# The scan of sixteen units: in two of them the product with C goes from VectorE to GpSimd

## The chip, the cores and the metric

The kernel runs on one core of a Trainium2 chip, as one program. The metric is the device time of that core in microseconds (us). The engines are named as in the profile: PE is TensorE, DVE is VectorE, ACT is ScalarE, POOL is GpSimd, and SP is the engine that issues the transfers.

## What is computed

The reference is four layers on a tensor of four images, 64 by 64 pixels and 128 channels. Layers 0 and 1 contain a selective scan in four directions over the 4096 pixels of an image; layers 2 and 3 are a graph of neighbours and a neighbourhood attention, and the change doesn't touch them. The scan is

```
def step(h, inp):
    d, u, b, c = inp
    dA = jnp.exp(d[..., None] * A)
    h = dA * h + (d * u)[..., None] * b[:, :, None, :]
    y = jnp.sum(h * c[:, :, None, :], axis=-1)
    return (h, y)
...
_, ys = lax.scan(step, h0, seq)
```

with 16 states `h` for each channel, 128 channels in layer 0 and 256 in layer 1. Everything is in fp32.

## The kernel before

There are twelve scan tasks, one for each image and tile of 128 channels (four in layer 0, eight in layer 1). A task runs over four directions and, in each, over four chunks of 1024 pixels. A chunk holds 128 channels x 16 states, 2048 recurrences, and is cut into sixteen units: a unit is 8 channels x 16 states on the 128 partitions, and 1024 pixels along the free dimension. That makes 256 units a task and 3072 in all. In the loop of `run` a unit `u` takes these steps, each issued some units ahead of the scan:

- `load` (six units ahead, L393): SP issues a transfer of 512 KB that spreads delta times x from DRAM over the states, into `dub` (four buffers).
- `times_b` (three ahead, L398): POOL multiplies `dub` by the repeated B into `dbu` (three buffers). The buffer of `dbu` for unit u+3 is the one that the scan of unit u reads last.
- `decay` (two ahead, L406 and L408): PE spreads delta into `da`, a tile of two banks in PSUM (two buffers), and ACT takes the exponential in place.
- `scan` (L418, L428, L430): DVE runs the recurrence over `da` and `dbu`, in place in `da`. In three of the four chunks of a direction it copies the last column into `state`, from where the next chunk's scan starts. Then it multiplies `da` by the repeated C into `hc` (six buffers, in SBUF). The buffer of `da` comes free with that multiplication.
- `add_up` (L453): for each group of four units PE gathers the four `hc` into the running sum `yps`, one half of the pixels in the slot of the group's last unit and the other half in the next slot.

The order of instructions on each engine is written out by the program as it stands; nothing reorders them later. Between the units, a planner (`Plan` and `Lane`) places two other streams: the preparation of the next chunk (`prepare`: delta, its exact split in three bf16 parts, delta times x; four POOL operations of 1024 columns a chunk) and a side stream of all the convolutions, norms and projections of layers 0 and 1. The planner keeps an estimate of when each of PE, ACT and POOL is free, `at`, charges each unit a fixed amount in `slot` (2.4 us on POOL), and lets a piece of the other streams in where its engine's estimate fits. DVE does almost nothing but the units. A one-off per task, `skip` (L441), is a small tensor-scalar operation on DVE from SBUF to SBUF.

After the last scan the rest of the program (the last image's end of layer 1, then layers 2 and 3) follows.

Of the kernel before, what the change touches and what calls it, by code (L numbers as in the profile page):

```python
# [26 lines left out]
NG = 16  # L27
# [87 lines left out]
class Plan:  # L115
# [37 lines left out]
    def slot(self, u, sums):  # L153
        at = self.at
        self.now = u * UNIT
        self.flush()
        at["PE"] = max(at["PE"], self.now) + 1.1
        at["ACT"] = max(at["ACT"], at["PE"]) + 1.1
        at["POOL"] = max(at["POOL"], self.now - 1.2) + 2.4
        at["PE"] += sums  # L160


# [71 lines left out]


NU = ND * NSTEP * NG
AHEAD = 22


class Scans:  # L240
# [140 lines left out]
    def unit(self, u):  # L381
        n, i = divmod(u, NU)
        step, g = divmod(i, NG)
        jj, j = divmod(g, 4)
        t = self.tasks[n]
        return t, step, jj, j, 4 * j + jj
# [23 lines left out]
    def scan(self, u):  # L410
        nc = self.nc
        t, step, jj, j, g = self.unit(u)
        back = t.steps[step][0] >= 2
        way = slice(None, None, -1) if back else slice(None)
        if g == 0:
            t.states[step] = self.tile("state", 2, shape=(P, NG))
        da, dbu = self.live.pop(("da", u)), self.live.pop(("dbu", u))
        nc.vector.tensor_tensor_scan(  # L418
            da[:, way],
            da[:, way],  # L420
            dbu[:, way],
            0.0 if step % NSTEP == 0 else t.states[step - 1][:, g : g + 1],
            ALU.mult,
            ALU.add,
        )
        if step % NSTEP < NSTEP - 1:
            end = 0 if back else TS - 1
            nc.vector.tensor_copy(t.states[step][:, g : g + 1], da[:, end : end + 1])  # L428
        hc = self.live["hc", u] = self.tile("hc", 6)
        nc.vector.tensor_mul(hc, da, t.prepared[step]["C"])  # L430

    def sum_so_far(self, u, i):

# [43 lines left out]
    def run(self, between):  # L477

        total = NU * len(self.tasks)
        first = self.tasks[0]  # L480
        for _ in self.fetch(first):
            pass
        for _ in self.prepare(first, 0):
            pass
        self.plan.start()
        pieces, fetch = Lane(self.plan, iter(())), iter(())
        for u in range(-6, total):
            if u >= 0:
                self.scan(u)
            if u >= 2:  # L490
                self.keep(u - 2)
            if 0 <= u + 3 < total:
                self.times_b(u + 3)
            if 0 <= u + 2 < total:
                self.decay(u + 2)
            if u >= 0 and u % NG in (2, 3):
                self.sum_so_far(u, u % NG - 2)
            if u >= 0 and u % 4 == 3:
                self.add_up(u, 0)
            if u > 0 and u % 4 == 0:  # L500
                self.add_up(u - 1, 1)
            self.plan.slot(u, (1.6 if u % 4 in (0, 3) else 0.0) + (2.1 if u % NG in (2, 3) else 0.0))
            ahead, rest = divmod(u + AHEAD, NG)
            if rest == 0:
                while pieces.step():
                    pass
                self.plan.flush("prep", "rep")
            if rest == 0 and 0 < ahead < total // NG:
                n, step = divmod(ahead, NU // NG)
                if step == 0:  # L510
                    self.plan.flush("side")
                    fetch = self.fetch(self.tasks[n])
                    for _ in range(self.tasks[n].W.nct):
                        next(fetch, None)
                pieces = Lane(self.plan, self.prepare(self.tasks[n], step))
            next(fetch, None)
            while (pieces.count < rest - 2 or pieces.fits()) and pieces.step():
                pass
            if u >= 0:
                n, i = divmod(u, NU)  # L520
                if self.later:
                    self.later.pop(0)()
                between(n, i)
            if 0 <= u + 6 < total:
                self.load(u + 6)
        self.add_up(total - 1, 1)
        self.keep(total - 1)
        while self.later:
            self.later.pop(0)()
# [508 lines left out]
def scan_layers(tc, C, nb, x_in, d0, s0, d1, s1, out):  # L1038

    nc = tc.nc  # L1040
    with ExitStack() as es:
# [19 lines left out]

        last = {g: group.index(g) * NU - AHEAD - 1 for g in range(1, len(groups))}
        last[len(groups)] = NU * len(tasks) - 16
        lane, current, credit = None, None, 0.0
# [396 lines left out]
def layer2(tc, C, nb, x_in, x_out, d_w, d_rel, d_v):  # L1461
    with ExitStack() as es:
# [11 lines left out]

        with tc.manual_schedule():
            run(each(E.statistics, 0, range(8)))
            E.roots([E.rstd])
            run(each(E.project, 0, range(6)))
            E.edge_row()
            run(each(E.statistics, 1, range(2)))  # L1480
            before = last = None
            for b in range(nb):
# [392 lines left out]
```

## Time and profile before

| | |
|---|---|
| median of 3 runs | 14536.44 us (14521.81 to 14541.9) |
| the profiled execution's own time | 14538.91 us |
| its span, first to last instruction | 14537.1 us |
| the scans, first start to last end | 202 to 11721 us |
| busy in the span: PE, DVE, ACT, POOL | 73%, 85%, 54%, 68% |
| one scan on DVE, with and without a start state | 2350 and 2290 ns |
| one product with C on DVE | 1218 ns |
| one product with B on POOL | 2356 ns |
| one exponential on ACT | 1089 ns |

Busy shares are averages over the whole span; the stage of the scans takes about four fifths of it, and the rest has other limits. In the rows of groups, "idle before" is the time that an engine stood still just ahead of those instructions, with the engine and tile whose completion ended the wait. A wait for several things is put down to the one that came last. In the text, "unit 5" means a unit whose number is 5 modulo 16.

### The profile page before, as it was taken

To read this page: it belongs to the slowest core of one execution; us is meant where nothing else is said; L and a number is where in the kernel's file an instruction comes from. 1 tells how busy PE (TensorE), PEld (TensorE's weight loads), DVE (VectorE), ACT (ScalarE), POOL (GpSimd) and SP (SyncE) were. 2 spreads that over 40 slices of the span, in tenths; PEclk is the share of its full clock that TensorE was granted. 3 is DMA by queue.
4 is the path that set the end of the run, shared out by engine and by line. 5 is a ranking of instruction groups with operands and counts; after the bars stand their busy time and mean duration, and the time that the engine had idled before them with its cause. 6 is when DMAs were issued, how large, how long until landed. Compare 5 with 4: busy or idle time off the path is not lost. (4 is left out here: it accounts for less than half of the span.)

```text
span 14537.1 us, 125468 instructions
## 1 busy us (share of the span) xinstructions
PE 10657.1 (73%) x36776; PEld 2733.4 (19%) x36776; DVE 12418.0 (85%) x10627; ACT 7829.5 (54%) x9243; POOL 9857.4 (68%) x4742
## 2 busy tenths in 40 slices
PE   5777777777767776667766777667777767777999
PEld 1111111111111111111111111111111112223555
DVE  4998899989999999989998999999999925565666
ACT  3665466645655466545655555555555545543555
POOL 4777788878877788778877888888888833341000
PEclk7666676666676766677666776667766678777999
DMA  6888888987889888988888878788787720002000
GB/s 164 215 215 218 202 211 214 222 219 205 210 227 219 208 211 206 228 204 206 211 207 215 204 193 204 194 204 203 195 206 193 194 80 22 25 13 49 13 13 8
DMA packets 854306, 2489.98 MB, mean 171 GB/s; under 512 B 143095, under 2 KB 164863, under 8 KB 845431
## 3 DMA queue, kind: packets, MB, share of 16 engines
q1 hardware_dynamic: 853623, 2481.97, 67.8%
q8 instruction: 295, 4.83, 0.1%
q14 instruction: 388, 3.18, 0.1%
HBM read 2060.21 MB, written 270.27 MB: 160 GB/s over the span
## 5 line engine op out<-in xcount | busy, mean ns | idle before, releaser
L398 POOL TENSOR_TENSOR dbu<-dub,repB 128x1024 f32<-128x1024 f32 x3072 | 7196.1, 2356 | 1649.0 <-DVE da L418 873.9
L418 DVE TENSOR_TENSOR_SCAN da<-da,state,dbu 128x1024 f32<-128x1024 f32 x2304 | 5415.0, 2350 | 376.9 <-ACT da L408 294.3
L408 ACT ACTIVATE da<-da,av 128x1024 f32<-128x1024 f32 x3072 | 3341.9, 1089 | 3765.6 <-PE da L406 3724.5
L406 PE MATMUL da<-dp,spread 96*128 96x512 bf16 x6144 | 2596.0, 516 | 2959.3 <-DVE hc L430 2922.7
L430 DVE TENSOR_TENSOR hc<-da,repC 128x1024 f32<-128x1024 f32 x3072 | 3740.2, 1218 | 40.5 <-DVE da L418 0.9
L453 PE MATMUL yps<-hc,gather 128*32 128x512 f32 x12288 | 2369.3, 854 | 2.3 <-DVE hc L430 2.3
L418 DVE TENSOR_TENSOR_SCAN da<-da,dbu 128x1024 f32<-128x1024 f32 x768 | 1759.0, 2290 | 321.4 <-POOL dbu L398 214.9
L406 PEld LDWEIGHTS <-spread 96*128 96x128 bf16 x6144 | 471.7, 107 | 6513.9 <-DVE hc L430 4173.5
L98 PE MATMUL ms<-d,wts 128*128 128x512 f32 (+3 forms) x900 | 701.7, 903 | 151.6 <-POOL d L98 107.9
L98 ACT ACT_TABLE_LOAD x600 | 769.8, 1283 | 79.3 <-DMA xcd<-o 63.8
L98 POOL TENSOR_TENSOR delta<-delta,low 128x1024 f32<-128x1024 f32 x192 | 452.2, 2355 | 460.0 <-ACT low L98 459.8
L98 PE MATMUL mp<-xd,dtw 8*128 8x512 f32 (+1 forms) x768 | 677.3, 976 | 43.7 <-DMA xd<-xdd 29.9
L98 ACT CAST parts<-delta 128x1024 bf16<-128x1024 f32 x384 | 399.8, 1041 | 304.1 <-POOL delta L98 291.7
L1411 POOL TENSOR_TENSOR acc<-acc,part 128x512 f32<-128x512 f32 x256 | 319.1, 1269 | 341.6 <-DVE part L1407 341.4
L446 PE MATMUL yps<-y,ident 128*128 128x512 f32 x576 | 531.6, 1018 | 3.5 <-ACT y L471 3.3
L453 PEld LDWEIGHTS yps<-hc,gather 128*32 128x32 f32 x12288 | 284.4, 128 | 1198.2 <-issue 1192.4
L98 POOL TENSOR_TENSOR low<-delta,xc 128x1024 f32<-128x1024 f32 x192 | 501.4, 2611 | 2.2
L1655 ACT ACTIVATE s<-s,nmax 128x512 f32<-128x512 f32 x512 | 366.2, 717 | 249.8 <-DVE nmax L1652 245.0
L1322 ACT ACTIVATE hid<-hid,relb 128x1024 f32<-128x1024 f32 x288 | 319.8, 1143 | 325.3 <-DVE hid L1317 322.6
L1317 DVE TENSOR_TENSOR hid<-cen,near 128x1024 f32<-128x1024 f32 x288 | 336.1, 1216 | 156.0 <-issue 66.6
L98 PE MATMUL ms<-pad,diag 96*32 96x504 f32 (+1 forms) x2304 | 425.1, 833 | 56.0 <-DMA pad<-xid 33.6
L98 ACT ACTIVATE low<-mp,av 128x512 f32<-128x512 f32 x384 | 263.7, 687 | 375.8 <-PE mp L98 371.2
(278 smaller groups left out, 11756.0 us busy)
## 6 DMA issues: line engine op xcount, KB each, us to landing
dub<-dud SPq DMA_DIRECT2D x3072, 512.0 KB
dp<-parts SPq DMA_DIRECT2D x2304, 64.0 KB
repB<-xdd SPq DMA_DIRECT2D x192, 512.0 KB
repC<-xdd SPq DMA_DIRECT2D x192, 512.0 KB
dud<-low SPq DMA_DIRECT2D x192, 512.0 KB
pad<-xid SPq DMA_DIRECT2D x192, 256.0 KB
szd<-o SPq DMA_DIRECT2D x96, 256.0 KB
xcd<-o SPq DMA_DIRECT2D x96, 256.0 KB
```

What stands on the lines that cost most here:

```text
L98: return call(*args, **kw)
L398: self.nc.gpsimd.tensor_mul(dbu, self.live.pop(("dub", u)), t.prepared[step]["B"])
L406: self.nc.tensor.matmul(da[:, cols], self.C.spread[:, jj, :], dp[:, j, cols], start=True, stop=True)
L408: self.nc.scalar.activation(da, da, AF.Exp, scale=t.W.a[:, at : at + 1])
L418: nc.vector.tensor_tensor_scan(da[:, way], da[:, way], dbu[:, way], 0.0 if step % NSTEP == 0 else t.states[step - 1][:, g : g + 1], ALU.mu ...
L430: nc.vector.tensor_mul(hc, da, t.prepared[step]["C"])
L446: self.nc.tensor.matmul(out, lhs, self.view(rhs, k, c, i, HALVES), start=True, stop=False)
L453: self.nc.tensor.matmul(self.live["yps"][32 * j : 32 * j + 32, cols], self.C.gather[:, jj, :], self.live["hc", v][:, cols], start=False, s ...
L1317: nc.vector.tensor_add(hid.rearrange("p i (r w) -> p (i r) w", w=HW), cen[pair].rearrange("p i (r w) -> p (i r) w", w=HW), self.near[m][s] ...
L1322: nc.scalar.activation(hid, hid, AF.Gelu, bias=self.relb[:, m, t : t + 1])
L1411: nc.gpsimd.tensor_add(acc, acc, part)
L1655: nc.scalar.activation(s[:, i, :], s[:, i, :], AF.Exp, bias=nmax[:, h : h + 1], accum_out=total[:, h : h + 1],)
```

## The change

In units 5 and 9 of each chunk, the scan writes its result to the `hc` tile in SBUF and not in place to `da` in PSUM. The state copy reads it there, and the product with C is done by POOL in place in `hc`. In all other units nothing is different. The loop issues `times_b` for unit u+3 ahead of the scan of unit u, and not after it, so that on POOL it stands ahead of the C product of unit u. The planner charges POOL 4.8 us in those two slots and not 2.4.

```
-        at["POOL"] = max(at["POOL"], self.now - 1.2) + 2.4
+        at["POOL"] = max(at["POOL"], self.now - 1.2) + (4.8 if u % NG in ASIDE else 2.4)
...
+ASIDE = (5, 9)
...
         da, dbu = self.live.pop(("da", u)), self.live.pop(("dbu", u))
+        hc = self.live["hc", u] = self.tile("hc", 6)
+        h = hc if u % NG in ASIDE else da
         nc.vector.tensor_tensor_scan(
-            da[:, way],
+            h[:, way],
             da[:, way],
             dbu[:, way],
...
             end = 0 if back else TS - 1
-            nc.vector.tensor_copy(t.states[step][:, g : g + 1], da[:, end : end + 1])
-        hc = self.live["hc", u] = self.tile("hc", 6)
-        nc.vector.tensor_mul(hc, da, t.prepared[step]["C"])
+            nc.vector.tensor_copy(t.states[step][:, g : g + 1], h[:, end : end + 1])
+        (nc.gpsimd if u % NG in ASIDE else nc.vector).tensor_mul(hc, h, t.prepared[step]["C"])
...
         for u in range(-6, total):
+            if 0 <= u + 3 < total:
+                self.times_b(u + 3)
             if u >= 0:
                 self.scan(u)
             if u >= 2:
                 self.keep(u - 2)
-            if 0 <= u + 3 < total:
-                self.times_b(u + 3)
```

## The prediction

> **What bounds the kernel now.** I read the page first, for the stages and the engines that the change loads differently.
>
> ```profile
> DVE 4998899989999999989998999999999925565666
> ACT 3665466645655466545655555555555545543555
> POOL 4777788878877788778877888888888833341000
> ```
>
> VectorE (DVE) stands at eight or nine tenths in 31 of the first 32 slices of 40. That is the scan stage, from 200 to 11720 us; the change touches nothing after it. Its busy times by engine, in the view by windows:
>
> ```profile
> 200.00:11720.00 11520.00, 8209.80 (x25364) 1702.57 (x25364) 10886.02 (x8459) 6362.36 (x6667) 9294.72 (x4271) 0.68 0.83 208
> ```
>
> The third busy figure is DVE, 10886 of 11520 us (94%); the fifth is GpSimd (POOL), 9295 (81%). Then the groups of POOL and of DVE in that stretch (busy us, mean ns of one, idle time just before them and who ended it):
>
> ```profile
> L398 POOL TENSOR_TENSOR dbu<-dub,repB 128x1024 f32<-128x1024 f32 x3072 | 7196.1, 2356 | 1649.0 <-DVE da L418 873.9 <-DMA dub<-dud 654.3 <-DVE hc L430 61.8
> ```
>
> ```profile
> L418 DVE TENSOR_TENSOR_SCAN da<-da,state,dbu 128x1024 f32<-128x1024 f32 x2304 | 5415.0, 2350 | 376.9 <-ACT da L408 294.3 <-POOL dbu L398 74.0 <-POOL pad L98 3.2
> L430 DVE TENSOR_TENSOR hc<-da,repC 128x1024 f32<-128x1024 f32 x3071 | 3739.0, 1218 | 40.5 <-DVE da L418 0.9
> L418 DVE TENSOR_TENSOR_SCAN da<-da,dbu 128x1024 f32<-128x1024 f32 x768 | 1759.0, 2290 | 321.4 <-POOL dbu L398 214.9 <-ACT da L408 102.2 <-POOL delta L98 3.4
> L428 DVE COPY state<-da 128x1 f32<-128x1 f32 x2304 | 364.4, 158 | 79.0
> L441 DVE TENSOR_SCALAR skip<-ident,dsum 128x128 f32<-128x128 f32 x12 | 18.8, 1569 | 0.0
> ```
>
> DVE's 0.7 ms of idle time before scans is split between the exponential (ACT da) and POOL's product (POOL dbu). So DVE bounds the stage and POOL is next: of POOL's idle 2225 us only 874 + 62 are spent waiting for DVE. A stretch of the timeline shows the pace and what is ready when:
>
> ```profile
> 8180.63 2.35 DVE L418 TENSOR_TENSOR_SCAN da<-da,state,dbu 128x1024 f32<-128x1024 f32 x1
> ...
> 8183.01 1.23 DVE L430 TENSOR_TENSOR hc<-da,repC 128x1024 f32<-128x1024 f32 x1
> ...
> 8184.15 2.35 DVE L418 TENSOR_TENSOR_SCAN da<-da,state,dbu 128x1024 f32<-128x1024 f32 x1
> ...
> 8184.30 1.03 PE L406 MATMUL da<-dp,spread 96*128 96x512 bf16 x2 [1.92 <-DVE hc L430]
> ...
> 8185.37 1.09 ACT L408 ACTIVATE da<-da,av 128x1024 f32<-128x1024 f32 x1 [2.87 <-PE da L406]
> ```
>
> Scan to scan is 3.52 us, of which the multiplication takes 1.14 (8183.01 to 8184.15). The end of a multiplication (8184.24) releases a `da` buffer; two matmuls and the exponential refill it by 8186.46, 2.22 us later. The scan running meanwhile ends at 8186.50. Now the multiplication after it covers another 1.1 us; without it that margin is nothing.
>
> [...] The `skip` instruction, SBUF to SBUF, takes 1569 ns on average against about 280 for one of its size (`wcen`, L1168) run while POOL is idle, and it ends as POOL passes from one instruction to the next:
>
> ```profile
> 6006.59 4.68 POOL L398 TENSOR_TENSOR dbu<-dub,repB 128x1024 f32<-128x1024 f32 x2
> ...
> 6010.11 1.25 DVE L441 TENSOR_SCALAR skip<-ident,dsum 128x128 f32<-128x128 f32 x1
> ...
> 6011.22 2.35 POOL L98 TENSOR_TENSOR low<-delta,xc 128x1024 f32<-128x1024 f32 x1
> ```
>
> The state copy reads PSUM and takes 157 to 164 ns in all 2304 cases. [...] no copy of that size from SBUF beside a busy POOL is in this trace. [...]
>
> **The change, part by part.** There are 192 chunks of sixteen units, so 384 units are affected.
>
> *DVE loses 384 multiplications.* At 1.14 us each that is 438 us, all on the path where DVE is the bound. But the next scan then needs its exponential a multiplication sooner. I paired the trace's rows unit by unit: from the end of a multiplication to the end of the exponential it releases the median is 2.87 us for unit 6 and 2.71 for unit 10, not 2.22, since sums and side matmuls get in PE's way, while a scan lasts 2.35. Cutting each gain to what the exponential and the product allow leaves 0.57 us a chunk after unit 5 and 0.63 after unit 9: 192 x 1.20 = **230 us** at most.
>
> *The scan writes SBUF instead of PSUM.* No row shows it. [...] I take zero.
>
> *The state copy reads SBUF.* It exists in three steps of four, 288 times. Lower bound: 158 ns as now, so nothing. Upper bound: it waits out POOL's instruction. Pairing rows, POOL is inside one at the end of scan 5 in 92% of chunks with 1.35 us left, and at the end of scan 9 in 60% with 1.08. The wait overlaps that for the exponential; taking the longer of the two, the saving becomes -0.06 us after unit 5 and 0.28 after unit 9. With POOL's new work unit 9 will look more like unit 5, so of the 230 about **20 us** stay. I take the upper bound[...]; the lower one is a rival.
>
> *POOL gains 384 multiplications* of 2356 ns, 905 us. Its share in the stage goes from 81 to 89%. Its waits for scans cover part; behind each new product stands the next `dbu`, and a scan behind that. POOL starts a `dbu` at most when the scan three units back has freed the buffer, so it can be about 5.8 us late before a scan waits. In units 2 to 12 it is already behind: the median start is 4.7 us after that scan's end at unit 5, 3.4 at unit 8, 2.7 at unit 9. Carrying 2.36 us from each new product through POOL's rows, with every idle gap absorbing its length and DVE's times left as they are, scans wait **119 us** longer; with DVE 0.6 us earlier per affected unit they wait 210. The changed charge of 4.8 in the planner will hold some side products back; I take off 20.
>
> *PE waits for `hc` from POOL.* The product of unit 5 is ready about 3.4 + 2.4 + 2.4 = 8.2 us after scan 5; the gathers of units 4 to 7 could begin at 7.2. In PE's queue behind them stand side matmuls and the matmuls of `da` 10, due at 10.7. Between nothing and 0.5 us a chunk; I take 0.15, **30 us**.
>
> *The order.* Issuing `times_b` for unit u+3 ahead of the scan changes POOL's queue alone in the affected units: the `dbu` product first, the C product behind it. Both wait for the same scan, so the move costs nothing. No DMA is moved past another; but a late `dbu` holds its `dub` buffer longer, and SP's next load stands behind that. DMA at 83% has room, and later products need later loads; I take zero. `hc` is taken a scan earlier from a ring of six, whose old content was gathered units before: zero.
>
> Sum against the profiled execution (14538.9 us, 1.8 around its span of 14537.1): -20 + 119 - 20 + 30 = about +110. The median shown, 14536.4, stands 2.5 lower, so 14646.
>
> **The rivals.**
> *The copy is not held (25%).* Then the 230 us stand against 210 of late products, of which the planner may save half, and 30 at PE: from +10 to -95, and with shorter PE waits -125. Mid -60: **14476**. [...] Against: POOL leaves little.
> *POOL becomes the bound (20%).* If POOL never waited for DVE again, the stage would last 11520 - 936 + 905 = 11489 us: 31 us is all that POOL allows as long as its waits for DMA (654) and for `low` (423) stay. POOL can run only three units ahead, so in units 13 to 1, where it waits for scans now, part of that wait remains; with half of it left, 468 - 31 = +437, and with some DMA waits swallowed about +250: **14786**. [...]
> *It does little (5%).* The exponential takes the whole gain and POOL's gaps its whole load: within 25 us of before.
>
> **How the numbers follow.** The first case has 50%. A measurement can tell 0.2%, 29 us, from no change. The first case is slower in 0.44 of all, level in 0.03 and faster in 0.03; the unheld copy faster in 0.18, level 0.04, slower 0.03; POOL as bound slower in 0.20; the last 0.03 level, 0.01 to each side. Slower 0.68, same 0.10, faster 0.22. The likeliest case alone spans 14530 (half the late products cured) to 14790 (POOL 0.75 us worse a chunk). The range over all reaches to the unheld copy and most of POOL as bound: 14430 to 14880.
>
> **What would show it.** In the profile after: 384 C products on POOL near 2356 ns and 2688 on DVE; state copies from `hc` lasting up to 2.5 us, over one on average (near 150 ns: the rival of the unheld copy); scans at units 6 and 10 waiting for ACT, unit 9 and the units after 12 for POOL `dbu`, in total some 120 us more than 289; POOL's share of the stage 87 to 90%. If copies are short, POOL waits grow by under 100 us and the stage falls below 11490, the forecast is wrong.

## The result, and the profile after

The changed kernel takes 14686.28 us (median of 4 runs, 14673.83 to 14692.09) against 14531.85 us before (4 runs): ratio 1.0105, 95% interval [1.0088, 1.0123], 154 us slower. Its profiled execution took 14673.83 us with a span of 14672.0; before, the span was 14537.1. So the two traces compared below differ by 135 us. The scans run from 204 to 11856 us, 134 us longer than before; what follows them is as long as before.

The page's rows by slices, for DVE and POOL:

```profile
DVE  4888889988999889888998999999999935565666
POOL 4887789978988798888987899999999943441000
```

DVE has lost some of its nines and POOL has gained them. The stage of the scans in the view by windows (PE, PEld, DVE, ACT, POOL busy):

```profile
200.00:11860.00 11660.00, 8178.09 (x25373) 1722.93 (x25374) 10477.66 (x8076) 6354.47 (x6667) 10155.91 (x4655) 0.69 0.82 206
```

DVE is busy for 408 us less (10478 against 10886), POOL for 861 more: 87% of the stage against 81%, nearly level with DVE's 90%. The groups of POOL, then of DVE, in that stretch (busy us, mean ns of one, idle just before them and its releasers):

```profile
L399 POOL TENSOR_TENSOR dbu<-dub,repB 128x1024 f32<-128x1024 f32 x3072 | 7185.6, 2356 | 1074.0 <-DMA dub<-dud 681.7 <-DVE da L421 334.7 <-DVE hc L432 27.0
L432 POOL TENSOR_TENSOR hc<-hc,repC 128x1024 f32<-128x1024 f32 x384 | 904.8, 2356 | 0.0
```

```profile
L421 DVE TENSOR_TENSOR_SCAN da<-da,state,dbu 128x1024 f32<-128x1024 f32 x2016 | 4741.5, 2352 | 710.9 <-ACT da L409 501.2 <-POOL dbu L399 190.5 <-POOL pad L98 5.3
L432 DVE TENSOR_TENSOR hc<-da,repC 128x1024 f32<-128x1024 f32 x2688 | 3273.0, 1218 | 37.6 <-DVE da L421 0.9 <-PE da L407 0.5
L421 DVE TENSOR_TENSOR_SCAN da<-da,dbu 128x1024 f32<-128x1024 f32 x672 | 1540.4, 2292 | 445.6 <-POOL dbu L399 268.6 <-ACT da L409 173.1 <-POOL delta L98 1.1
L421 DVE TENSOR_TENSOR_SCAN hc<-da,state,dbu 128x1024 f32<-128x1024 f32 x288 | 674.7, 2343 | 66.3 <-ACT da L409 40.1 <-POOL dbu L399 25.7
...
L421 DVE TENSOR_TENSOR_SCAN hc<-da,dbu 128x1024 f32<-128x1024 f32 x96 | 219.1, 2282 | 24.2 <-POOL dbu L399 10.4 <-ACT da L409 9.2 <-POOL delta L98 4.4
L431 DVE COPY state<-hc 128x1 f32<-128x1 f32 x288 | 44.4, 154 | 9.8
L443 DVE TENSOR_SCALAR skip<-ident,dsum 128x128 f32<-128x128 f32 x12 | 13.2, 1102 | 0.0
```

The change did what it says: 384 C products on POOL at 2356 ns, 2688 left on DVE. The row to look at first is `state<-hc`: 154 ns, against 158 from PSUM. **The copy is not held by POOL**: in the trace, 259 of these 288 copies lie wholly inside one POOL instruction, and none took longer than 157 ns. `skip` still is held: eleven of the twelve ended 81 to 87 ns after the POOL instruction that was running when they began, and the twelfth, begun between two POOL instructions, took 278 ns. Then the idle time before scans: 710.9 + 445.6 + 66.3 + 24.2 = 1247 us, against 698 before. In both figures some 187 us are one wait, that of the very first scan for its product; most of it lies ahead of the stage. Inside the stage it is 1060 against 512. Who ends it, in the view of waits of DVE in this stage (us in total, times, longest), first before, then after:

```profile
DVE da L418 <- ACT da L408: 396.5, 309, 13.1
DVE da L418 <- POOL dbu L398: 288.8, 67, 186.2
```

```profile
DVE da L421 <- ACT da L409: 674.3, 501, 14.5
DVE da L421 <- POOL dbu L399: 459.1, 221, 187.5
DVE hc L421 <- ACT da L409: 49.3, 23, 7.6
DVE hc L421 <- POOL dbu L399: 36.1, 40, 3.3
```

Waits for exponentials have grown by 327 us (to 723.6) and those for POOL's product by 206 (to 495.2; without the first scan's wait, from 103 to 308). From the first scan's start to the last one's end DVE is busy for 411 us less and idle for 545 more, and this makes the 134 us.

A stretch of the timeline of the changed kernel shows both kinds of delay. The scan into `hc` is that of unit 9:

```profile
8228.67 2.35 DVE L421 TENSOR_TENSOR_SCAN hc<-da,state,dbu 128x1024 f32<-128x1024 f32 x1
...
8230.92 2.33 POOL L399 TENSOR_TENSOR dbu<-dub,repB 128x1024 f32<-128x1024 f32 x1
8231.05 0.15 DVE L431 COPY state<-hc 128x1 f32<-128x1 f32 x1
8231.07 0.59 PE L407 MATMUL da<-dp,spread 96*128 96x512 bf16 x2 [0.33 <-DVE hc L421]
...
8233.22 2.11 POOL L98 TENSOR_TENSOR delta<-delta,parts 128x1024 f32<-128x1024 f32 x1
8233.28 2.36 DVE L421 TENSOR_TENSOR_SCAN da<-da,state,dbu 128x1024 f32<-128x1024 f32 x1 [2.08 <-POOL dbu L399]
...
8235.30 4.68 POOL L399 TENSOR_TENSOR dbu<-dub,repB 128x1024 f32<-128x1024 f32 x2
8235.36 1.04 ACT L98 CAST parts<-delta 128x1024 bf16<-128x1024 f32 x1 [4.62 <-POOL delta L98]
...
8236.31 1.08 ACT L409 ACTIVATE da<-da,av 128x1024 f32<-128x1024 f32 x1
...
8237.67 2.36 DVE L421 TENSOR_TENSOR_SCAN da<-da,state,dbu 128x1024 f32<-128x1024 f32 x1 [0.71 <-POOL dbu L399]
...
8239.94 2.38 POOL L432 TENSOR_TENSOR hc<-hc,repC 128x1024 f32<-128x1024 f32 x1
...
8246.76 2.36 DVE L421 TENSOR_TENSOR_SCAN da<-da,state,dbu 128x1024 f32<-128x1024 f32 x1 [1.82 <-POOL dbu L399]
```

The copy runs at its usual length inside a POOL instruction (8230.92 to 8233.25). Scan 10 waits 2.08 us for its `dbu`. The added product of unit 9 starts only at 8239.94, 8.9 us after its scan, since POOL is behind; the `dbu` after it are late, and scan 13 waits 1.82 us (the last row). Between them stands the way in which late POOL work becomes a late exponential: PE has filled the `da` of unit 11 by 8231.66, but the exponential starts at 8236.31, behind a cast for which ACT had waited 4.62 us on a POOL product of the preparation. It ends at 8237.39. The `dbu` of unit 11 comes at about 8237.65, later still, so the view puts this scan's wait of 0.71 us down to POOL; the exponential alone would have held it for about 0.4 of them.

### The profile page after: what moved, and what is told of

It reads as the page before. It is cut to its first block, busy times and chain, and to the rows that moved or that the text cites. A ratio compares the mean times of both kernels' runs of the same rounds, so it can differ in the third digit from the quotient of the medians.

```text
span 14672.0 us, 125565 instructions
## 1 busy us (share of the span) xinstructions
PE 10622.4 (72%) x36776; PEld 2752.4 (19%) x36776; DVE 12007.5 (82%) x10243; ACT 7821.6 (53%) x9243; POOL 10718.5 (73%) x5126
## 5 line engine op out<-in xcount | busy, mean ns | idle before, releaser
L399 POOL TENSOR_TENSOR dbu<-dub,repB 128x1024 f32<-128x1024 f32 x3072 | 7185.6, 2356 | 1074.0 <-DMA dub<-dud 681.7
L421 DVE TENSOR_TENSOR_SCAN da<-da,state,dbu 128x1024 f32<-128x1024 f32 x2016 | 4741.5, 2352 | 710.9 <-ACT da L409 501.2
L407 PE MATMUL da<-dp,spread 96*128 96x512 bf16 x6144 | 2549.3, 509 | 2953.5 <-DVE hc L432 2858.5
L432 DVE TENSOR_TENSOR hc<-da,repC 128x1024 f32<-128x1024 f32 x2688 | 3273.0, 1218 | 37.6 <-DVE da L421 0.9
L421 DVE TENSOR_TENSOR_SCAN da<-da,dbu 128x1024 f32<-128x1024 f32 x672 | 1540.4, 2292 | 445.6 <-POOL dbu L399 268.6
L432 POOL TENSOR_TENSOR hc<-hc,repC 128x1024 f32<-128x1024 f32 x384 | 904.8, 2356 | 0.0
L421 DVE TENSOR_TENSOR_SCAN hc<-da,state,dbu 128x1024 f32<-128x1024 f32 x288 | 674.7, 2343 | 66.3 <-ACT da L409 40.1
```

The source lines that it names most:

```text
L399: self.nc.gpsimd.tensor_mul(dbu, self.live.pop(("dub", u)), t.prepared[step]["B"])
L407: self.nc.tensor.matmul(da[:, cols], self.C.spread[:, jj, :], dp[:, j, cols], start=True, stop=True)
L421: nc.vector.tensor_tensor_scan(h[:, way], da[:, way], dbu[:, way], 0.0 if step % NSTEP == 0 else t.states[step - 1][:, g : g + 1], ALU.mul ...
L432: (nc.gpsimd if u % NG in ASIDE else nc.vector).tensor_mul(hc, h, t.prepared[step]["C"])
```

## The experiments

Two stories can explain the result beside "POOL is late": the planner's new charge moves other work to worse places, or the scans come too early for their exponentials. Every ratio below is against runs of the kernel before on the same chip.

**The planner's charge alone.**

```
-        at["POOL"] = max(at["POOL"], self.now - 1.2) + 2.4
+        at["POOL"] = max(at["POOL"], self.now - 1.2) + (4.8 if u % NG in ASIDE else 2.4)
```

> The kernel before, with nothing of the change but the planner's charge of 4.8 us on POOL in units 5 and 9. Theory A (POOL is late: its 384 added products delay the products with B behind them, and the gathers): POOL gets no work here, so within 0.2% of before (29 us). Theory B (the planner's new charge moves the side pieces to places where they hold up PE and ACT): most of the measured loss is here already, slower than before by 70 to 200 us. Theory C (the scan of units 6 and 10 comes too early for its exponential, so that nothing is gained): within 0.2% of before.

Measured: 14577.91 us, ratio 1.0033 [1.0021, 1.0046], 47 us slower. A small part of the loss, between the figures of A and C (within 29 us) and that of B: B is right that the charge costs, and wrong that it is most. The waits of DVE in this kernel:

```profile
DVE da L419 <- ACT da L409: 453.5, 333, 12.5
DVE da L419 <- POOL dbu L399: 275.3, 53, 188.1
```

POOL's part has shrunk by 13 us, as the charge is there to do; the waits for exponentials have grown by 57. That the side pieces, moved to give POOL room, now stand in front of exponentials is the likely way; it was not traced piece by piece.

**The change without the charge.**

```
-        at["POOL"] = max(at["POOL"], self.now - 1.2) + (4.8 if u % NG in ASIDE else 2.4)
+        at["POOL"] = max(at["POOL"], self.now - 1.2) + 2.4
```

> The whole change, but the planner charges POOL 2.4 us in every unit as before. Theory A: the charge holds side products back behind the added ones and helps; without it slower than the change by 0 to 100 us (14690 to 14790). Theory B: faster than the change by 70 us or more (below 14615). Theory C: as the change, within 30 us.

Measured: 14659.25 us, ratio 1.0086 [1.0072, 1.0100]. The interval overlaps that of the change itself, so that the charge costs 27 us here too is likely, not settled. Theory A's "the charge helps" is not borne out, and B's recovery of 70 us doesn't come; it is inside C's 30 us of the change, which this run alone can't exclude. Without the charge 128 us of loss remain, and those have another cause.

**The product on POOL cut short, with the charge and without it.**

```
+        if u % NG in ASIDE:
+            nc.gpsimd.tensor_mul(hc[:, 0:32], h[:, 0:32], t.prepared[step]["C"][:, 0:32])
+        else:
+            nc.vector.tensor_mul(hc, h, t.prepared[step]["C"])
```

> The whole change, order and charge too, but the product on POOL covers only 32 of the 1024 columns (the other columns of hc in units 5 and 9 stay without their factor C). DVE keeps its gain and POOL's added work nearly vanishes. Theory A: the gain of some 230 us appears, less what the short instructions cost: faster than before by 130 to 230 us (14300 to 14400). Theory B: the planner's order is that of the change, so still slower than before by 0 to 100 us. Theory C: at most 50 us faster than before.

> The short product on POOL (32 of 1024 columns; the others keep no factor C in units 5 and 9), without the new charge. If the charge costs 47 us wherever it is made, this is 136 us faster than before (14395, 14375 to 14415); if its cost was that of the same waits for exponentials which the early scans make anyway, it is as with the charge (14440, within 20).

Measured: with the charge 14442.09 us, ratio 0.9940 [0.9927, 0.9954], 89 us faster: short of A's 130, past C's 50, and the opposite of B. Without the charge 14408.35 us, 0.9917 [0.9904, 0.9931], 124 us faster and inside the range of the first alternative. So DVE's relief, with 97 us of short POOL products still in it, is worth 124 us, and the rest of POOL's product (807 us of its time), in units 5 and 9 and with no charge, costs 128 + 124 = 252 us. With the charge it is the change against the first of these kernels: 244 us. Both kernels also contain the scan into SBUF and the earlier `hc`, so these don't explain the loss.

**POOL's load alone.** DVE keeps its products; POOL does the product with B twice in units 9 and 13, which is 384 added products in front of the same instructions.

```
         self.nc.gpsimd.tensor_mul(dbu, dub, t.prepared[step]["B"])
+        if (u - 4) % NG in ASIDE:
+            self.nc.gpsimd.tensor_mul(dbu, dub, t.prepared[step]["B"])
```

> DVE keeps all its products, as before; order and charge are those of the change, and POOL does the product with B of units 9 and 13 twice, so that it has the same 384 added products just ahead of the same instructions. Theory A: slower than before by 80 to 200 us (119 was worked out in the prediction), the time going to scans that wait for POOL. Theory B: slower than before, and by as much as the kernel with the charge alone. Theory C: within 30 us of before, as DVE is the bound.

Measured: 14716.35 us, ratio 1.0127 [1.0114, 1.0141], 185 us slower; less the 47 of the charge alone, 138. Its waits of DVE for POOL, where the second row is that of the repeated product:

```profile
DVE da L424 <- POOL dbu L400: 289.2, 68, 187.3
...
DVE da L424 <- POOL dbu L402: 98.6, 70, 5.6
```

Together 388 against 275 with the charge alone: 113 of the 138 are direct waits for POOL. DVE is the busiest engine of the stage (10892 us of 11690, 93%, against POOL's 10174, 87%), and still the added POOL work sets the time: theory A. It excludes B (as much as the charge alone) and C (within 30 us of before). That about the same load, with the charge in both, costs 244 where DVE is relieved and 138 where it isn't fits the prediction's two figures, 210 and 119: what DVE gains, it loses again by arriving before POOL.

**Another place.** The change without the charge, with one line different:

```
-ASIDE = (5, 9)
+ASIDE = (12,)
```

> The change with one unit a chunk, 12, in place of 5 and 9, and without the new charge. Theory A1 (what costs is the place: POOL has no idle time left in units 2 to 12 and much of it in units 13 to 1): the gain of 192 products on DVE, some 0.5 to 0.8 us each, stays, and POOL's added 452 us fall into its waits: faster than before by 40 to 120 us (14410 to 14490). Theory A2 (POOL has no room for any added product): half of what the change without the charge lost, slower than before by about 64 us (14595).

> Unit 12 alone without the charge, with the product on POOL cut to 32 of 1024 columns (the others keep no factor C in unit 12). Theory A1: POOL's whole product costs nearly nothing in this place, so within 30 us of the kernel with the whole product (14410 to 14460). Theory A2: it costs about half of the 252 us that it cost in units 5 and 9, so 90 us or more faster (below 14355).

Measured: 14444.17 us, ratio 0.9939 [0.9925, 0.9952], **89 us faster than before**, with the whole product. With the product cut to 32 columns 14433.7 us, 0.9933 [0.9920, 0.9945]. So the other 403 us of POOL's product cost about 10 us in this place, which the intervals can't tell from nothing, against 252 for 807 us in units 5 and 9. POOL's groups say where it went; first the cut product's kernel, then the whole product's:

```profile
L399 POOL TENSOR_TENSOR dbu<-dub,repB 128x1024 f32<-128x1024 f32 x3072 | 7192.4, 2355 | 1562.4 <-DMA dub<-dud 703.4 <-DVE da L421 688.3 <-DVE hc L421 112.6
```

```profile
L399 POOL TENSOR_TENSOR dbu<-dub,repB 128x1024 f32<-128x1024 f32 x3072 | 7185.3, 2353 | 1227.9 <-DMA dub<-dud 606.8 <-DVE da L421 460.2 <-DVE hc L421 107.6
...
L432 POOL TENSOR_TENSOR hc<-hc,repC 128x1024 f32<-128x1024 f32 x192 | 451.5, 2351 | 0.0
```

The idle time before `dbu` falls by 335 us, 228 of it from waits for scans: the product lies mostly in time that POOL had spent waiting. Counted unit by unit, 286 of the 335 stood before the products with B of units 0 and 1, the first ones behind the added product. This is theory A1. Behind unit 5 there is less of such time: in the kernel before, POOL stands idle for 215 us in all before the four products 9 to 12, and for 705 before the products 0 to 3 behind unit 12. Behind unit 9 there is more, 817 us before the products 13 to 15 and 0, but by then POOL has the delay from unit 5 as well. A kernel with unit 5 or unit 9 alone was not run, so what each of them costs by itself is not known.

**Other units.** `ASIDE = (12, 14)`, `(13,)` and `(8, 12)`, all without the charge.

> As the kernel with unit 12, with units 12 and 14. Theory A1: faster than before by 60 to 200 us (14330 to 14470), unless the second product, which ends as the next chunk's preparation begins on POOL, is late for it. Theory A2: slower than before by about 130 us, as much as the change without the charge.

> The change without the charge, in unit 13 alone, the second of its group. POOL has idle time there as in unit 12. If POOL's idle time alone decides: as unit 12, 14420 to 14480. If the gather's wait for a late hc matters too, one unit less of cover: 20 to 60 us slower than unit 12 (14460 to 14510).

> The change without the charge, in units 8 and 12 (each the first of its group of four for the gather). Theory A1 with the gather (place on POOL and place in the group decide): unit 12 keeps its 89 us; unit 8 lies where POOL is still behind, but its hc isn't needed for two more units, so between 40 lost and 60 won on top: 14380 to 14490. Theory A2' (a second product a chunk always loses, as with unit 14): slower than unit 12 alone by 50 us or more (over 14495).

Measured: units 12 and 14, 14500.38 us, 0.9977 [0.9970, 0.9985], so 56 us worse than 12 alone: a miss of A1's range, whose own reservation was the next chunk's preparation. The trace points to another cause. Unit 14 is the third of its group, and PE's gather waits for its `hc`, first at the matmul, then at the weight load:

```profile
PE yps L455 <- POOL hc L432: 138.4, 53, 8.9
```

```profile
PEld yps L455 <- POOL hc L432: 303.4, 160, 9.8
```

In the changed kernel the second of these is 45 us. DVE feels it in two places: against unit 12 alone, waits for exponentials before scan 2 of the next chunk grow by 102 us (PE starts that unit's matmuls about 1 us later on average), and scan 14 waits 80 us for PE to free an `hc` buffer. Unit 13, the second of its group as 5 and 9 are: 14458.86 us, 0.9955 [0.9942, 0.9967], within the range of "idle time alone decides", 15 us from unit 12, which these intervals can't tell apart. Units 8 and 12: 14470.68 us, 0.9959 [0.9947, 0.9972], inside the range of the place on POOL and in the group; it gives no more than unit 12 alone. None of these beats unit 12 alone. But units 8 and 12 give DVE and POOL the same 384 products to trade as units 5 and 9 do, also without the charge, and take 189 us less (14470.68 against 14659.25): the place counts at the same load.

**The order of the two products on POOL undone,** the change without the charge otherwise: `times_b(u + 3)` issued behind the scan again.

> The change without the charge, and with the product with B of unit u+3 issued after the scan of unit u again, so that on POOL it stands behind the added product with C of units 5 and 9. Theory D1 (late products with B are what costs): units 8 and 12 now get theirs 2.4 us later, while units 9 and 13 get them as before; slower than with the new order by 10 to 100 us (14670 to 14760). Theory D2 (the late hc, for which PE's gathers wait, is what costs): hc comes 2.4 us earlier, so faster than with the new order by 30 to 100 us (14560 to 14630).

Measured: 14697.07 us, 1.0110 [1.0094, 1.0125], 38 us slower than with the new order (1.0086), the intervals just overlapping. DVE's waits for POOL's `dbu` grew by 36 us, from 427 + 78 us (scans of the other units, and of 5 and 9) to 513 + 28. It points to D1, the late products with B, and away from the late `hc`.

**A ring of four for `dbu`, one less for `hc`.**

```
-        dbu = self.live["dbu", u] = self.tile("dbu", 3)
+        dbu = self.live["dbu", u] = self.tile("dbu", 4)
...
-        hc = self.live["hc", u] = self.tile("hc", 6)
+        hc = self.live["hc", u] = self.tile("hc", 5)
```

> The change without the charge, with four buffers for dbu in place of three, and five for hc in place of six to make room. Theory B1 (POOL is late because the ring lets it work only three units ahead, so that its idle time in units 13 to 1 can't be used for units 2 to 12): it can now get a unit further ahead, and most of the 140 us at least of late products go: 80 to 200 us faster than the change without the charge (14460 to 14580). Theory B2 (POOL is held by its own work and by its transfers): within 40 us of it (14620 to 14700).

Measured: 15242.66 us, 1.0489 [1.0475, 1.0504], 710 us slower than before: neither theory. The kernel can't decide between them, since the room was taken from a ring that the scan into `hc` now needs earlier:

```profile
DVE hc L421 <- PE yps L455: 1009.9, 341, 10.7
```

Scans 5 and 9 wait for the gather of the unit five back, 1010 us in all. Whether a fourth `dbu` buffer alone would let POOL use its idle time for units 2 to 12 stays open.

## Why the prediction was right or wrong

The forecast was slower, +110 us; it is +154, inside the range. The direction and the bound (POOL behind DVE, late in units 2 to 12) were right. **The likeliest case's own mechanism was not**: a gain that was wrongly written off stood against losses that were left out, so that the figure came near is in good part luck.

- **The state copy: wrong.** This is the step that failed. The upper bound was chosen, on the showing of `skip` (1569 ns against about 280 of an operation of its size): a copy of one element per partition would be held for POOL's instruction, and all but 20 of the 230 us would go. It takes 154 ns, also inside a POOL instruction. The case that came true is the one with an unheld copy, which had been put at -60 us. Of the signs against the forecast, the short copies came, but the waits for POOL did not stay under 100 us more and the stage did not shrink. `skip` has 128 columns and the copy one; the row was not near enough to decide.
- **The gain at units 5 and 9: right.** Pairing the starts of scans as in the prediction, the 192 intervals from scan 5 to scan 6 sum to 585 us against 703, those from scan 9 to scan 10 to 598 against 716: 236 us, worked out 230. Idle time before scans 6 and 10 grew by 197, where 438 - 230 = 208 were expected.
- **Late products with B: right in size.** 119 with DVE's times unchanged (measured 138, of which 113 are waits for POOL), 210 with DVE earlier: waits for POOL grew by 206 in the changed kernel. The 289 us that the prediction names as the waits before contain the first scan's 186; its 0.7 ms of DVE's idle time in the stage is 0.5 for the same reason. The full cost of POOL's length, 244 to 252, contains what late POOL work does through ACT and PE as well.
- **The planner's charge: wrong sign.** Taken as -20, and as saving up to half the late products in the rival. It costs 47 us alone, 34 with the short product (14442 against 14408) and, as far as the intervals tell, 27 in the change.
- **Exponentials in the other fourteen units: left out.** By the pairing (which of a scan's two inputs came last), idle time before scans that a late exponential ended grew by some 320 us, only some 125 of it at units 6 and 10. Outside these two units it grew by 196 us in the change, by 148 without the charge, and by 63 with the short product and no charge. So some 50 of it go with the charge and some 85 with the full length of POOL's product. The last 63 are there with almost no added POOL work: a gain in two units is partly given back at the next late exponential. For the part of POOL's length, late side products that hold ACT and PE are the likely way. Without the charge, ACT's waits for `delta` products went from 292 to 437 us and PE's for `d` from 108 to 224, as these rows of the change without the charge show:

```profile
ACT parts L98 <- POOL delta L98: 436.9, 219, 13.5
```

```profile
PE ms L98 <- POOL d L98: 224.4, 87, 15.2
```

  One exponential that is late behind such a cast is seen in the timeline above; how much of the 85 us comes this way was not tried by itself.
- **PE's wait for `hc`, 30 us: right for units 5 and 9** (45 us of waits at the weight load, 3 at the matmul), and the point that decides for a unit later in its group (14).
- **The moved `times_b`: right** that it costs nothing; undone, it loses some 38 us.
- **The scan into SBUF, zero: right.** 2343 ns with a start state against 2352 into PSUM. The `hc` taken earlier costs nothing either: no scan of the change waits for a gather. POOL's waits for its loads, also put at nothing, went from 654 to 682 us; whether the change made them is not shown.
- **POOL becomes the bound, +250:** POOL's share of the stage, 87%, stayed below DVE's 90%. But its reason, that POOL's waits for scans can't all be used, holds: after the change 335 us of them are left, while scans wait for POOL elsewhere in the same chunk.

In one sum against the profiles: 236 us gained at two intervals, and 370 lost in the other fourteen, some 140 of it in waits for POOL's product and some 200 in waits for exponentials. The other 67 us of POOL's growth lie at units 6 and 10, and are already taken off the 236.

## What to carry to other kernels

Before moving work to a less busy engine, ask at which point of the cycle it is idle, and not only how much: the length of the product cost 252 us in units 5 and 9 together and about 10 in unit 12, and the same number of products turned from 0.9% slower in units 5 and 9 to 0.4% faster in units 8 and 12. In this kernel POOL was behind through part of the cycle and set the time there, though DVE's mean share was higher (90% of the stage against 87%); whether another buffer would let it use its idle time elsewhere stayed open. And the relieved engine arrived early at the units behind as well (with the short product and no charge, waits for exponentials grew by 63 us in the other fourteen units): count what their inputs leave of the gain, and price a planner's reordering as a cost until it is measured (here 47 us by itself).

## What the runs showed of the hardware that was not expected

A copy of one fp32 element per partition from SBUF to SBUF on VectorE ran 288 times in 153 to 157 ns while GpSimd was busy for 87% of the stage, for 8090 of its 10156 us with products of two tiles: 259 of the 288 lie wholly inside one POOL instruction, 212 of them with more than 0.5 us of it left when they began. A tensor-scalar operation of 128 columns took 1102 ns on average in the same trace, and eleven times of twelve ended 81 to 87 ns after POOL's instruction did. What sets the two apart, no run shows. And a GpSimd product of 1024 columns takes 2356 ns whether its output is a third tile or in place in its first input.
